# Two transformer blocks with self and cross attention: the opening of the kernel, with ScalarE's queue loading batch 1 and GpSimd normalising it

## The chip, the cores and the metric

The kernel runs on one core of one Trainium2 chip. The metric is the device time of one execution in microseconds (us). A core has five engines that run their own instruction streams side by side: TensorE (PE, matrix products), VectorE (DVE), ScalarE (ACT), GpSimd (POOL) and SyncE (SP), which here only starts transfers. They wait for each other through semaphores. Each stream is executed strictly in the order in which it was written, so what stands behind a waiting instruction waits too. A transfer (DMA) is started by an instruction in the stream of SP, ACT or POOL, and is then carried out by 16 DMA engines that all streams share.

## The reference

The input x has 4 batches of 512 tokens with 320 features each, and every batch has a context of 1601 tokens with 192 features. Two layers are applied, each with the same three blocks:

```
h1 = layernorm(x);  x = attention(h1, h1)      @ Wo + bo + x     # 20 heads of 16, self attention
h2 = layernorm(x);  x = attention(h2, context) @ Wo + bo + x     # cross attention, 1601 keys
h3 = layernorm(x);  a, g = split(h3 @ W1 + b1)
x  = (a * gelu(g)) @ W2 + b2 + x
```

A layernorm takes the mean and the variance of a token over its 320 features, multiplies by the inverse root and then applies a gain and a bias. An attention is softmax(q k / 4) v by heads. All of it is in float32.

## The kernel before, in words

**Tiles.** Tokens lie on 128 partitions, four blocks of 128 to a batch. A *unit* is one batch and one group of four heads, so a self attention has 4 x 5 units and unit 0 to 4 are batch 0, unit 5 the first of batch 1. For the scores, four heads share the array of TensorE, 32 rows each.

**The work of one self unit.** First its queries and keys are projected (`both`, L898, in two halves of 24 matmuls each). ACT copies the result out of PSUM. Each number is then split into a high and a low part (`split`, L825, two POOL instructions; unit 0 uses ACT and DVE instead, L919 and L920), and a transfer moves the parts to where the scores want them (`at_once`, L1609, runs the moves, L876: keys on SP's queue, queries alternating). Next come the *maxima*: four rounds of eight matmuls (L1076) into PSUM, with one DVE reduction (L1087) for each of the 16 tiles. `max_end` (L1152) turns these maxima into rows on DVE and sends them off with four small transfers (L1171, into `nrows`). Only then does the unit's *main part* run (`main`, L1311): four chunks c of keys, each with 12 matmuls for four heads (L1324, the third of each head adds the row of maxima), four exponentials on ACT (L1334), and the product with the values (L1350). The values themselves come from `values` (L1025, 24 matmuls for one chunk and one part of the heads).

**What sets the order.** The order of the instructions is written out by the Python program. In the main parts a planner does it: beside each chunk it gives out the following units' rounds of maxima (`give`, L1639), and after the chunk it takes projections, values and norms from chains by due times and a credit (`steps`, L487). A unit's maxima have to be finished by the chunk c = 1 of the unit before it; what is left by then is added as extra rounds. The eight PSUM banks are handed out by an estimate of when each comes free (`bank`, L413).

**The opening**, L1683 to L1724, is written out by hand, with `start["on"]` true. It loads x of batch 0, the first norm's gain and bias, the weights of queries, keys and values, two bias rows and x of batch 1, all on SP's queue, in this order. Ten warm-up matmul instructions (`warm(5)`, L431) run on TensorE meanwhile. Batch 0's norm follows: statistics on DVE (`stats`, L556), an inverse root by a bit trick and three Newton steps (`guess_root` L518, `better_root` L530, small DVE instructions on 128x4 numbers), the normalisation (`plain`, L620, twelve DVE instructions), and the turning by TensorE (`turn`, L634, twelve transposes and three copies out of PSUM that apply gain and bias; it ends with four POOL additions, `biased`, L617). Then come the projection of unit 0 and its transfer, the projection of unit 1, all of batch 1's statistics, root and normalisation on DVE, and then unit 0's maxima. Between its four rounds stand the two halves of unit 2's projection and some values. Two rounds of unit 1's maxima and four more sets of values end the opening; then unit 0's main part begins. Batch 1's turning is left to the planner, which places it after chunk c = 0 of unit 0.

Of the kernel before, what the change touches and what calls it, by code (L numbers as in the profile page):

```python
# [23 lines left out]
P = 128  # L24
# [54 lines left out]
def kernel(ctx: ExitStack, tc: tile.TileContext, x, context, ws, out):  # L79
# [96 lines left out]

    def load_x(b):

        src = x[b].rearrange("(c p) d -> p c d", p=P)

        def part(t):
            dma(out=xs[b][:, t], in_=src[:, t])
            loaded[b] = clock["round"] if t == NQ - 1 else 1 << 30

        return [lambda t=t: part(t) for t in range(NQ)]
# [38 lines left out]

    def load_row(t, v):
        dma(out=t, in_=v.rearrange("(o d) -> o d", o=1).to_broadcast([P, D]))

    def load_bias(l, i):
        if i > 2:
            l, i = l + 1, i - 3  # L230
        if l < L:
            load_row(brow[(3 * l + i) % 2], ws[l][("o1_b", "o2_b", "ff_b2")[i]])

# [283 lines left out]

    def guess_root(var):  # L518
# [6 lines left out]
        nc.vector.tensor_scalar(y.bitcast(I32), z.bitcast(I32), -1, 0x5F3759DF, ALU.mult, ALU.add)  # L525
# [4 lines left out]
    def better_root(h, y, z):  # L530


        eng = nc.vector if start["on"] else nc.gpsimd
        eng.tensor_tensor(z, y, y, ALU.mult)
        eng.tensor_tensor(z, z, h, ALU.mult)
        eng.tensor_scalar(z, z, 1.5, None, ALU.add)
        eng.tensor_tensor(y, y, z, ALU.mult)
# [13 lines left out]
    def add_norm(l, b, i, put, done, due):  # L551
# [13 lines left out]
        def root(step):  # L565
            if step == 0:
                s["root"] = guess_root(s["mv"][:, :, 1])
                s["rstd"] = s["root"][1]
            for _ in range(step + 1):
                better_root(*s["root"])  # L570
            s["round"] = clock["round"]
# [48 lines left out]
        def plain(t):  # L620
            if t == 0:
                s["hn"] = one.tile([P, DB, NQ, SLOT], F32, tag="hturned", name="hturned").rearrange("p k t w -> p (k t w)")
            for k, at, n in HK:
                w = n // SLOT
                (nc.vector if start["on"] else nc.gpsimd).tensor_scalar(
                    s["hn"][:, t * D + at : t * D + at + n].rearrange("p (d k) -> p k d", k=w),
                    xb[:, t, at : at + n].rearrange("p (k d) -> p k d", k=w),
                    s["mv"][:, t, 0:1], s["rstd"][:, t : t + 1], ALU.subtract, ALU.mult,
                )
            if start["on"]:  # L630
                busy("dve", 0.45)
            s["round"] = clock["round"]

        def turn(k, at, n):  # L634
            if k == 0:
                place()
            ps = bank("hps")
            for t in range(NQ):
                nc.tensor.transpose(ps[:n, t * P : (t + 1) * P], s["hn"][:, t * D + at : t * D + at + n], ident)
            written(0.5, ps)  # L640
# [511 lines left out]
    def max_end(u):  # L1152
# [14 lines left out]
        def rows():  # L1167
            for i in range(P // SLOT):
                part = slice(i * SLOT, (i + 1) * SLOT)
                queue = (nc.sync, nc.scalar, nc.gpsimd, nc.sync)[i] if start["on"] else nc.sync  # L1170
                queue.dma_start(out=slots[:, :, part], in_=turned[part, :])  # L1171
# [601 lines left out]
```

## Time and profile before

| | |
|---|---|
| median of 3 runs | 2921.99 us (2918.47 to 2926.42) |
| the profiled execution's own time | 2916.39 us |
| its span in the profile | 2914.6 us |
| TensorE busy | 2860.1 us (98% of the span) |
| DVE busy | 1975.7 us (68%) |
| ACT busy | 1950.2 us (67%) |
| POOL busy | 1299.4 us (45%) |
| mean granted TensorE clock | 0.995 |

The profile comes from one execution. A row of the timeline or of the chain of waits has a start and a duration in us, the engine, the line of the kernel and what was written from what. "x8" means that eight instructions were merged into one row. An engine name with a q (SPq, ACTq) is that engine issuing a transfer. A row of the windows has the stretch, its length, the busy time of PE, PEld (the loading of weights into the array), DVE, ACT and POOL, then the granted TensorE clock as a share of full speed, the busy share of the DMA engines and their rate. PE's busy time includes time in which a matmul is held up inside its queue, so "busy" is not "at full speed".

### The profile page before, as it was taken

The page shows a single profiled execution, that of the slowest core. Times are in us where ns is not written, and L with a number is a line of the kernel's source. Part 1 is how long each engine was busy: PE and PEld are TensorE (multiplying, and loading weights), DVE is VectorE, ACT ScalarE, POOL GpSimd, SP SyncE. Part 2 cuts the span into 40 slices and gives each one's busy share as a digit, 9 for nine tenths or more (in the row PEclk, how much of TensorE's full clock was granted, in tenths as well). Part 3 has the DMA queues.
Part 4 walks back from the last instruction along what each step waited for, and adds up shares of the span by engine and source line. Part 5 has one row for each costly group of instructions (what it writes and reads, how often), then busy time and mean ns, then how long its engine had stood idle before and what let it go on. Part 6 is the DMA issues. An engine that isn't in the chain of part 4 may idle for free.

```text
span 2914.6 us, 83287 instructions
## 1 busy us (share of the span) xinstructions
PE 2860.1 (98%) x35018; PEld 1545.0 (53%) x35018; DVE 1975.7 (68%) x3752; ACT 1950.2 (67%) x4033; POOL 1299.4 (45%) x1409
## 2 busy tenths in 40 slices
PE   8999999999999999999999999999999999999999
PEld 4445555555555555355554555555555555544554
DVE  7777888788788878323257678787778878862221
ACT  3777678888888888500138776788888888893000
POOL 3656345555645545211125653455455464551100
PEclk8999999999999999999999999999999999999999
DMA  4444223232132222200113432222221122122000
GB/s 106 114 121 102 72 71 97 58 89 60 48 96 59 55 54 63 85 17 11 36 45 88 109 99 67 61 64 57 54 66 47 50 73 60 45 65 67 23 21 13
DMA packets 163495, 188.59 MB, mean 65 GB/s; under 512 B 61989, under 2 KB 109105, under 8 KB 163121
## 3 DMA queue, kind: packets, MB, share of 16 engines
q1 hardware_dynamic: 162616, 181.69, 24.4%
q8 instruction: 275, 4.51, 0.6%
q10 hardware_dynamic: 472, 1.58, 0.2%
q14 instruction: 100, 0.81, 0.1%
q0 software_dynamic: 32, 0.00, 0.0%
HBM read 55.76 MB, written 29.36 MB: 29 GB/s over the span
## 4 chain that ended last, share of the span: by engine, by line
PE 88%; DVE 4%; POOL 4%; DMA 2%; issue 1%; ACT 1%; SPq 0%; POOLq 0%; ACTq 0%; DVEq 0%
PE av L1350 22%; PE st L1324 20%; PE fps L1435 10%; PE sps L1076 9%; PE yps L1542 6%; PE vps L1035 5%; PE kps L972 4%; PE ops L1250 3%; PE qkps L908 3%; PE fps L1495 3%; DVE nmax L1087 2%; PE qps L947 2%; PE sps L1101 1%; POOL o L1370 1%; DVE pm L1087 1%
## 5 line engine op out<-in xcount | busy, mean ns | idle before, releaser
L1334 ACT ACTIVATE pr<-st 128x512 f32<-128x512 f32 (+1 forms) x2720 | 1405.0, 603 | 321.4 <-PE st L1324 292.0
L1087 DVE TENSOR_REDUCE pm<-sps 128x1 f32<-128x512 f32 (+1 forms) x1920 | 1148.3, 660 | 244.6 <-PE sps L1076 239.0
L1370 POOL TENSOR_TENSOR o<-o,vo 128x512 f32<-128x512 f32 x576 | 739.9, 1285 | 930.3 <-ACT vo L1369 909.7
L1076 PE MATMUL sps<-kT,q 32*128 32x450 f32 (+1 forms) x4800 | 870.6, 422 | 8.1 <-DMA q<-halves 4.4
L1324 PE MATMUL st<-q,kT 32*128 32x512 f32 (+1 forms) x5120 | 788.9, 419 | 0.8 <-ACT o L1364 0.4
L1350 PE MATMUL av<-pr,vals 128*32 128x512 f32 (+1 forms) x5440 | 734.2, 606 | 27.3 <-ACT pr L1334 5.4
L1324 PEld LDWEIGHTS st<-q,kT 32*128 32x128 f32 (+1 forms) x5120 | 447.0, 180 | 293.0 <-issue 112.7
L1324 PE MATMUL st<-nrows,ones 32*128 32x512 f32 (+1 forms) x2720 | 560.6, 398 | 4.5 <-DMA nrows<-turned 4.4
L1087 DVE TENSOR_REDUCE nmax<-sps 128x1 f32<-128x512 f32 x640 | 397.2, 682 | 118.0 <-PE sps L1076 114.2
L1076 PEld LDWEIGHTS sps<-kT,q 32*128 32x128 f32 x4800 | 434.0, 184 | 67.1 <-ACT pr L1334 11.7
L1369 ACT COPY vo<-av 128x512 f32<-128x512 f32 x576 | 351.7, 611 | 14.7 <-PE av L1350 8.7
L1506 ACT ACTIVATE gl<-fps,b 128x512 f32<-128x512 f32 x80 | 54.8, 687 | 408.8 <-PE fps L1495 299.1
L1435 PE MATMUL fps<-hT,w 128*128 128x512 f32 x640 | 283.1, 597 | 0.0
L1350 PEld LDWEIGHTS av<-pr,vals 128*32 128x32 f32 (+1 forms) x5440 | 111.0, 108 | 300.3 <-DVE pm L1087 185.2
L1324 PEld LDWEIGHTS st<-nrows,ones 32*128 32x128 f32 (+1 forms) x2720 | 262.3, 180 | 14.5 <-DMA nrows<-turned 6.1
L1507 DVE SCALAR_TENSOR_TENSOR hid<-fps,b,gl 128x512 f32<-128x512 f32 x80 | 59.7, 748 | 248.1 <-ACT gl L1506 246.0
L1435 PEld LDWEIGHTS fps<-hT,w 128*128 128x128 f32 x640 | 119.2, 190 | 155.1 <-issue 152.2
L1542 PE MATMUL yps<-w,hid 128*128 128x320 f32 x640 | 175.7, 434 | 0.0
L1542 PEld LDWEIGHTS yps<-w,hid 128*128 128x128 f32 x640 | 120.5, 190 | 56.3 <-ACT gl L1506 5.3
L1250 PEld LDWEIGHTS ops<-wo,aT 112*32 112x32 f32 (+1 forms) x3072 | 98.2, 110 | 59.2 <-issue 28.5
L1250 PE MATMUL ops<-wo,aT 112*32 112x160 f32 (+1 forms) x3072 | 123.8, 299 | 3.7 <-POOL aT L1232 2.7
L1111 DVE TENSOR_REDUCE pm<-sps 128x4 f32<-128x508 f32 x160 | 98.9, 680 | 37.5 <-PE sps L1101 34.8
(89 smaller groups left out, 2453.7 us busy)
## 6 DMA issues: line engine op xcount, KB each, us to landing
kT<-stages SPq DMA_DIRECT2D x80, 400.5 KB
oway<-o SPq DMA_DIRECT2D x80, 256.0 KB
q<-halves SPq DMA_DIRECT2D x80, 256.0 KB
q<-halves SPq DMA_DIRECT2D x27, 512.0 KB
kT<-halves SPq DMA_DIRECT2D x40, 256.0 KB
aT<-oway SPq DMA_DIRECT2D x32, 224.0 KB
rT<-rway SPq DMA_DIRECT2D x32, 224.0 KB
hT<-hturned SPq DMA_DIRECT2D x96, 64.0 KB
```

What stands on the lines that cost most here:

```text
L972: nc.tensor.matmul(ps[(i * GT + f) * SLOT : (i * GT + f + 1) * SLOT, :w], lhsT=wk2[:, k, u.g * GD + f * SLOT : u.g * GD + (f + 1) * SLOT], ...
L1035: nc.tensor.matmul(ps[f : f + m, :w], lhsT=u.kvT[:n, k, at + f : at + f + m], rhs=wv[:n, k, h0 * DH : h1 * DH], start=(k == 0), stop=(k == ...
L1076: nc.tensor.matmul(own[0][:, :w], lhsT=u.queries(slice(j * SLOT, (j + 1) * SLOT), e, t), rhs=u.kT[j * SLOT : (j + 1) * SLOT, u.k0 + at : u ...
L1087: nc.vector.tensor_reduce(to, own[0][:, :w], AX.X, ALU.max)
L1250: nc.tensor.matmul(ps[f : f + m, : D // 2], lhsT=aT[:n, k, f * NQ + t * SLOT : f * NQ + t * SLOT + m], rhs=wo[:n, k, cols], start=(k == 0) ...
L1324: nc.tensor.matmul(own[0][:r, :], lhsT=ones[rows, :r] if e == 2 else u.keys(rows, c), rhs=u.rows[rows, :] if e == 2 else u.queries(rows, e ...
L1334: nc.scalar.activation(p[:r], own[0][:r], AF.Exp)
L1350: nc.tensor.matmul(ps[j * SLOT : (j + 1) * SLOT, :], lhsT=columns_of[:r, head : head + SLOT], rhs=pr.pop((c, j))[:r, :], start=True, stop= ...
L1369: nc.scalar.copy(vo, ps)
L1370: nc.gpsimd.tensor_tensor(u.o, u.o, vo, ALU.add)
L1435: nc.tensor.matmul(ps, lhsT=w1[:, k, i * FF + c * P : i * FF + (c + 1) * P], rhs=natural(u.hT[:, k]), start=start, stop=stop,)
L1542: nc.tensor.matmul(ps[:, :D], lhsT=hid[c][:, t * P : (t + 1) * P], rhs=w2[:, c, :], start=(c == 0), stop=(c == NHC - 1),)
```

## The change

Everything that changes is in the opening and in three helpers.

- The loads: x of batch 0 is started on SP's and ACT's queues in turn. x of batch 1 and the two bias rows are started on ACT's queue right behind. SP's queue goes from batch 0's tokens directly to gain, bias and weights. The four transfers of unit 0's row of maxima use SP and ACT only, two each (before: SP, ACT, POOL, SP).
- The root: on DVE, the last two instructions of a Newton step become one. For batch 1 the Newton steps run on POOL, with `guess_root`'s last instruction.
- The normalisation of batch 1 (`plain`) runs on POOL, and all three of its copies out of PSUM on ACT.
- The warm-up has seven matmuls, not five, and three small matmuls whose result nothing reads stand between the first four transposes of batch 0.
- The order: batch 1's statistics and root are written before unit 1's projection, and three sets of values behind it, before unit 1's transfer. Batch 1's normalisation follows that transfer. Unit 0's maxima then have unit 2's projection between them but no values. `max_end` of unit 0 stands ahead of unit 2's transfer. One round of unit 1's maxima is done in place of two, and batch 1's turning is done in the opening. Three sets of values and one round of maxima go over to unit 0's main part.

```diff
-    def load_x(b):
+    def load_x(b, queues=(nc.sync,)):
...
-            dma(out=xs[b][:, t], in_=src[:, t])
+            queues[t % len(queues)].dma_start(out=xs[b][:, t], in_=src[:, t])
...
-        eng = nc.vector if start["on"] else nc.gpsimd
+        eng = nc.vector if start["on"] and not b else nc.gpsimd
         eng.tensor_scalar(h, a, -0.5, None, ALU.mult)
...
+        eng = nc.vector if start["on"] and not b else nc.gpsimd
         eng.tensor_tensor(z, y, y, ALU.mult)
         eng.tensor_tensor(z, z, h, ALU.mult)
+        if eng is nc.vector:
+            eng.scalar_tensor_tensor(y, z, 1.5, y, ALU.add, ALU.mult)
+            return
...
-                (nc.vector if start["on"] else nc.gpsimd).tensor_scalar(
+                (nc.vector if start["on"] and not b else nc.gpsimd).tensor_scalar(
...
+            idle = bank("wps") if start["on"] and k == 0 and not b else None
             for t in range(NQ):
                 nc.tensor.transpose(ps[:n, t * P : (t + 1) * P], s["hn"][:, t * D + at : t * D + at + n], ident)
+                if idle is not None and t + 1 < NQ:
+                    nc.tensor.matmul(idle[:, :P], lhsT=ident, rhs=fill[:, :P], start=True, stop=True)
...
-            if start["on"] and k == 1:
+            if start["on"] and k == 1 and not b:
...
-                queue = (nc.sync, nc.scalar, nc.gpsimd, nc.sync)[i] if start["on"] else nc.sync
+                queue = nc.scalar if start["on"] and i % 2 else nc.sync
...
-    now(load_x(0))
+    now(load_x(0, (nc.sync, nc.scalar)))
+    now(load_x(1, (nc.scalar,)))
+    load_bias(0, 0, nc.scalar)
+    load_bias(0, 1, nc.scalar)
     now(load_self(0))
-    load_bias(0, 0)
-    load_bias(0, 1)
-    now(load_x(1))
...
-    warm(5)
+    warm(7)
...
     add_values(units[0])
+    for _ in range(NQ + 2):
+        run("norm")
     run("proj")
     run("proj")
-    for _ in range(2 * NQ + 2):
+    for _ in range(3):
+        run("values")
+    at_once(units[1])
+    for _ in range(NQ):
         run("norm")
-    at_once(units[1])
     add_proj(units[2])
...
-    for chain in ("proj", "proj", "values", None):
+    for chain in ("proj", "proj", None, None):
...
-    at_once(units[2])
-    run("values")
     max_reduce(first)
     max_end(first)
+    at_once(units[2])
+    second = units[1]
+    second.pairs = max_pairs(second)
+    round_of(second.pairs[0].popleft()[1] + second.pairs[1].popleft()[1])
+    for _ in range(3):
+        run("norm")
     loads.extend(load_x(2))
...
-    second = units[1]
-    second.pairs = max_pairs(second)
-    for _ in range(2):
-        round_of(second.pairs[0].popleft()[1] + second.pairs[1].popleft()[1])
-        run("values")
-        run("values")
```

More of the change, by code (lines that the diff above doesn't have):

```diff
@@ L223, in load_columns, with load_row, load_bias @@
         return [lambda c=c: column(*c) for c in chunks]
-    def load_row(t, v):
-        dma(out=t, in_=v.rearrange("(o d) -> o d", o=1).to_broadcast([P, D]))
-    def load_bias(l, i):
+    def load_row(t, v, queue):
+        queue.dma_start(out=t, in_=v.rearrange("(o d) -> o d", o=1).to_broadcast([P, D]))
+    def load_bias(l, i, queue=nc.sync):
         if i > 2:
@@ L231, in load_bias @@
         if l < L:
-            load_row(brow[(3 * l + i) % 2], ws[l][("o1_b", "o2_b", "ff_b2")[i]])
+            load_row(brow[(3 * l + i) % 2], ws[l][("o1_b", "o2_b", "ff_b2")[i]], queue)
     def load_norm(l, i):
@@ L516, in until, with guess_root @@
             run(name)
-    def guess_root(var):
+    def guess_root(var, b):
         a, h, y, z = (two.tile([P, NQ], F32, tag=f"root{i}", name=f"root{i}") for i in range(4))
@@ L525, in guess_root, with better_root @@
         nc.vector.tensor_scalar(y.bitcast(I32), z.bitcast(I32), -1, 0x5F3759DF, ALU.mult, ALU.add)
-        eng = nc.vector if start["on"] else nc.gpsimd
+        eng = nc.vector if start["on"] and not b else nc.gpsimd
         eng.tensor_scalar(h, a, -0.5, None, ALU.mult)
         return h, y, z
-    def better_root(h, y, z):
-        eng = nc.vector if start["on"] else nc.gpsimd
+    def better_root(h, y, z, b):
+        eng = nc.vector if start["on"] and not b else nc.gpsimd
         eng.tensor_tensor(z, y, y, ALU.mult)
         eng.tensor_tensor(z, z, h, ALU.mult)
+        if eng is nc.vector:
+            eng.scalar_tensor_tensor(y, z, 1.5, y, ALU.add, ALU.mult)
+            return
         eng.tensor_scalar(z, z, 1.5, None, ALU.add)
@@ L566, in root @@
             if step == 0:
-                s["root"] = guess_root(s["mv"][:, :, 1])
+                s["root"] = guess_root(s["mv"][:, :, 1], b)
                 s["rstd"] = s["root"][1]
             for _ in range(step + 1):
-                better_root(*s["root"])
+                better_root(*s["root"], b)
             s["round"] = clock["round"]
@@ L637, in turn @@
             ps = bank("hps")
+            idle = bank("wps") if start["on"] and k == 0 and not b else None
             for t in range(NQ):
                 nc.tensor.transpose(ps[:n, t * P : (t + 1) * P], s["hn"][:, t * D + at : t * D + at + n], ident)
+                if idle is not None and t + 1 < NQ:
+                    nc.tensor.matmul(idle[:, :P], lhsT=ident, rhs=fill[:, :P], start=True, stop=True)
+            if idle is not None:
+                busy("act", 0.0, idle)
             written(0.5, ps)
```

## The prediction

> **What bounds the kernel now.** I read the page first.
>
> ```profile
> span 2914.6 us, 83287 instructions
> PE 2860.1 (98%) x35018; PEld 1545.0 (53%) x35018; DVE 1975.7 (68%) x3752; ACT 1950.2 (67%) x4033; POOL 1299.4 (45%) x1409
> ```
>
> TensorE bounds nearly all of the span. The change touches nothing but the opening, so it can win only time that TensorE loses there. How much that is, the windows of the opening show (us; then PE, PEld, DVE, ACT, POOL busy; granted clock; DMA).
>
> ```profile
> 8.95:12.36 3.41, 1.18 (x4) 0.61 (x5) 3.34 (x14) 0.00 (x0) 0.00 (x0) 0.99 0.70 202
> 12.36:15.77 3.41, 3.41 (x25) 2.19 (x27) 1.10 (x3) 1.55 (x2) 0.00 (x0) 0.51 0.51 154
> 19.19:22.60 3.41, 1.13 (x24) 0.37 (x12) 3.17 (x10) 0.95 (x2) 3.33 (x5) 0.99 0.77 185
> 23.00:43.00 20.00, 18.23 (x184) 9.53 (x184) 17.97 (x47) 1.75 (x5) 4.29 (x6) 0.50 0.35 87
> 43.00:57.00 14.00, 13.45 (x184) 7.65 (x180) 10.52 (x19) 8.14 (x17) 1.68 (x3) 1.00 0.04 12
> ```
>
> The clock falls to half twice, each time behind a stretch of 3.4 us in which TensorE worked about a third of the time. The second fall lasts 20 us. In those 20 us DVE is busy for 17.97, so it holds TensorE up as well. The chain of waits says what comes first:
>
> ```profile
> 9.06 0.17 DVE root L537
> 9.52 2.60 DVE hturned L625 x9
> 12.17 2.11 PE hps L639 x9
> 14.27 3.50 PE qkps L908 x48
> 18.82 5.86 DMA q<-halves
> 24.77 1.23 PE sps L1076 x8
> ```
>
> DVE's root and normalisation, the turning, unit 0's projection and a transfer of 5.86 us lead to unit 0's first maxima at 24.77. The timeline has the rest:
>
> ```profile
> 25.33 3.39 DVE L625 TENSOR_SCALAR hturned<-x,mv,root 128x128 f32<-128x128 f32 x12
> 28.61 4.86 DVE L1087 TENSOR_REDUCE nmax<-sps 128x1 f32<-128x512 f32 x8
> 39.62 0.17 DVE L1155 TENSOR_REDUCE nmax<-nmax 128x16 fp32r<-128x16 f32 x1
> 40.29 1.45 SPq L1171 DMA_DIRECT2D nrows<-turned  x2
> 48.64 1.53 PE L639 MATMUL hps<-ident,hturned 128*128 128x128 f32 x12
> 49.49 2.11 ACT L647 ACTIVATE hT<-hps,lnb,lng 128x512 f32<-128x512 f32 x3
> 50.10 0.49 PE L1324 MATMUL st<-q,kT 32*128 32x512 f32 x2
> 52.28 1.06 PE L1350 MATMUL av<-pr,vals 128*32 128x512 f32 x8
> 53.28 0.74 PE L1076 MATMUL sps<-kT,q 32*128 32x512 f32 x8
> 53.95 2.80 PE L908 MATMUL qkps<-hT,wqk 128*32 128x256 f32 x48
> 54.05 2.48 DVE L1087 TENSOR_REDUCE nmax<-sps 128x1 f32<-128x512 f32 x4 [0.52 <-PE sps L1076]
> 56.68 0.49 PE L1324 MATMUL st<-q,kT 32*128 32x512 f32 x2
> ```
>
> Batch 1's normalisation holds DVE until 28.7, so the 16 reductions begin 3.8 us behind the first maxima. They end at 39.6. The scores of unit 0's chunk c = 1 start at 50.10, those of c = 2 at 56.68.
>
> **Where to measure.** By the planner's rules both kernels have done the same work when c = 2 begins. In the kernel before, the planner turns batch 1 behind c = 0. In the changed one that is done, and the credit goes to three sets of values; unit 3's projection isn't ready there in either, and follows behind c = 1. Of unit 1's maxima one round more is left, which `give` adds at c = 1 beside the extra round of unit 2 that the trace shows at 53.28. Units, rounds and due times are then equal, so I take the rest as unchanged, and the gain is 56.68 less the new start of c = 2.
>
> **Up to the first maxima.** Each small DVE instruction of the root takes 0.2 us from start to start (9.06 to 9.26 ends the last); three fewer save 0.6. The warm-up gets four matmul instructions on top of its ten:
>
> ```profile
> 1.53 6.48 PE L435 MATMUL wps<-fill,ident 128*128 128x512 f32 x10 [1.53 <-POOL scales L119]
> ```
>
> It ended at 8.0; four more are 2.6 at the row's mean and fewer at full clock, so it ends between 9.5 and 10.6, and with the three fillers TensorE is idle for little over 1 us ahead of the last transposes. I take it that the first fall of the clock goes. Nine transposes then cost 9 x 1.53/12 = 1.15 in place of 2.11 (saved 0.96), and 48 projection matmuls 2.80 in place of 3.50 (0.70). If the clock falls all the same, only 0.6 is left; the sum is 0.6 to 2.3. Against it stand the new neighbours on the DMA engines:
>
> ```profile
> 6.52 1.88 SPq L214 DMA_DIRECT2D wqk<-in_L_xattn_q_dram  x3
> 12.29 1.07 SPq L226 DMA_DIRECT2D brow<-in_L_xattn_o_b_dram  x2
> 17.58 3.35 POOL L618 TENSOR_TENSOR x<-x,brow 128x320 f32<-128x320 f32 x4 [11.17 <-DVE halves L920]
> ```
>
> SP issues the weights about 1 us earlier (two of batch 0's moves leave it, and an issue takes 0.63 here), but they now share the engines with batch 1's tokens and the bias rows. The latter were slow: issued at 12.29, first used at 17.58. Late weights cost 0 to 1.5; I take 0.3, since the last key weights (6.52 and six issues, less 1) are issued by 9.3 and wanted near 13. ACT's eight issues, by the same 0.63, end near 6, and ACT has nothing else to do until the turning, so they cost nothing. The transfer of 5.86 stays. First maxima: 24.77 - 2.26 + 0.3 = 22.8.
>
> TensorE has unit 1's projection and three sets of values ahead of them, so it is idle for about 2 us, where it was from 20.3 (19.19 and the 1.13 of that window) to 24.77.
>
> **Unit 0's maxima.** DVE is free by then. A reduction follows its matmuls by 0.8 (53.28 to 54.05), so the 16 run from 23.6 at 0.61 each (4.86 for eight), 9.8 in all, to 33.4; `max_end` takes 0.67 (39.62 to 40.29), to 34.1. Two row transfers on each queue take 1.45 to issue and some 1.8 to land, by the one landing that the view of transfers times:
>
> ```profile
> nrows<-turned POOLq DMA_DIRECT2D x1, 4.0 KB, 1.8
> ```
>
> The rows are there at 37.3.
>
> **POOL's chain.** This is what the change adds. Batch 1's later sisters show the durations on POOL:
>
> ```profile
> 96.38 0.20 POOL L534 TENSOR_TENSOR root<-root 128x4 f32<-128x4 f32 x1
> 96.66 0.20 POOL L535 TENSOR_TENSOR root<-root,root 128x4 f32<-128x4 f32 x1
> 104.01 4.39 POOL L625 TENSOR_SCALAR hturned<-x,mv,root 128x128 f32<-128x128 f32 x6
> 109.82 2.22 POOL L625 TENSOR_SCALAR hturned<-x,mv,root 128x128 f32<-128x128 f32 x3
> 111.92 0.62 POOL L827 CAST halves<-halves 128x512 fp32r<-128x512 f32 x1
> 112.63 1.28 POOL L828 TENSOR_TENSOR halves<-halves 128x512 f32<-128x512 f32 x1
> 115.13 2.25 POOL L625 TENSOR_SCALAR hturned<-x,mv,root 128x128 f32<-128x128 f32 x3
> ```
>
> The root's 13 instructions follow each other at 0.29, 3.8 in all. The normalisation is 4.39 + 2.22 + 2.25 = 8.9, where DVE took 3.39. A split is 2.0 (111.92 to the end at 113.91). What runs ahead of it and what it let go before:
>
> ```profile
> 21.80 1.11 DVE L525 TENSOR_SCALAR root<-root 128x4 int32<-128x4 int32 x1
> 22.92 0.57 ACTq L876 DMA_DIRECT2D q<-halves  x1
> ```
>
> DVE's third and last instruction of what stays on it of batch 1's root began at 21.80. It moves by 2, so POOL gets the root at about 19.9. POOL then runs: root to 23.7, split of unit 1 to 25.7, normalisation to 34.6, split of unit 2 to 36.5. Unit 1's transfer leaves 2.8 later than the 22.92 of before, and lands by 31.6, still ahead of its first maxima (banks come free near 31 to 33.6). Behind unit 2's split stands ACT: its queue holds unit 2's query transfer (0.6, to 37.1) and then batch 1's three copies out of PSUM (2.11, to 39.2). Only then are there enough banks for the first round of unit 0's main part, four tiles of scores and four of maxima. So POOL and ACT, not the rows at 37.3, set this start. In the kernel before, POOL was off this path.
>
> **From there to c = 2.** Round c = 0 ends at 40.1. Three sets of values follow: two of 192 columns and one of 128, by this row 2.14 and, by its columns, 0.71:
>
> ```profile
> 64.21 2.14 PE L1035 MATMUL vps<-wv,hT 128*32 128x192 f32 x48
> ```
>
> Together 2.9, to 43.0. Then c = 1 at its old 2.2 (50.10 to 52.28), the product with the values 1.0, unit 1's extra round 0.7, unit 3's projection 2.7, unit 2's extra round 0.7: 50.3. Before, that extra round stood ahead of the projection, which covered its four reductions (2.48). Now c = 2 follows directly and wants their banks, which I cost at 1.2. c = 2 begins at 51.5: a gain of 5.2 at full clock.
>
> **The clock behind the gap.** Between 31 and 39 TensorE has only one round of maxima and twelve transposes, some 2.5 us of work, less than the third of a window that went ahead of both falls. So I expect half clock at 39. It came back twice in the trace: after 3.4 us of steady work at 12.36, but only after 20 us from 23, where TensorE waited for DVE in every window. The values are a steady stream, so I take the shorter: 4 us at half clock, 2.0 lost. Bounds: 0 and 20 us, 0 to 10 lost. A rule that speaks here is in the Trainium skill, "TensorE: Matmul & The Clock Gate", in the part on the HAM clock gate: one idle window of about 3.4 us throttles, one busy window of the same length releases. By it the loss would be 1.7, an estimate. The first fall and its end agree with it; the 20 us do not, as TensorE counted as busy for 18.23 of them.
>
> **Sum.** 5.2 - 2.0 = 3.2. For the profiled execution that is 2916.4 - 3.2 = 2913.2. It stands 5.6 below the median of the runs, 2921.99, from which I take the same: 2918.8.
>
> **Rivals.**
> (1) The clock doesn't fall at 39, or the lost time is in waits anyway: the gain is 5.2 to 6.4 (without the stall at c = 2), 2916. For it speaks that c = 0 waits for ACT; against it, the light work from 31 on.
> (2) Slower: half clock stays, as it did from 23 to 43, because unit 0's main part starts with DVE one round of maxima behind and TensorE waits for it at c = 1. The gain of 5.2 is gone when it lasts more than 10.4 us; at 20 us the loss is 10, and the kernel is 4.8 slower, 2926.8. Against it: in the main parts from 43 on the clock was 1.00 throughout.
> (3) The change doesn't do what it says at the front: bias rows and tokens delay the weights by 1.5 and the first fall of the clock comes all the same. Then 2.3 - 0.6 + 1.2 = 2.9 are lost again and the gain is 0.3: 2921.7.
> (4) POOL isn't in the way, because the planner's bank choice doesn't tie the first scores to batch 1's copies. Then DVE alone bounds c = 2: 36 reductions and one `max_end` from 23.6, 36 x 0.61 + 0.7, to 46.3, and c = 2 some 0.8 later. The gain is 9.6: 2912.4.
> (5) POOL's and DVE's instructions hold each other up. One row speaks for it, the DVE root instruction at 21.80, which took 1.11 while POOL split unit 1's numbers, where its neighbours take 0.2. If each of batch 1's twelve POOL instructions held up a reduction by half of its 0.74, 4.4 would be lost on the maxima, of which 1.7 is slack up to POOL's own end: gain 0.5, 2921.5. Against it: reductions took the same 0.62 in the main part (2.48 for four from 54.05).
>
> **Chances.** The forecast has 0.50, (1) 0.18, (2) 0.10, (3) 0.09, (4) 0.08, (5) 0.05. The likeliest's own range is 2914 to 2923, three on either side for the weights and the clock, and 1.5 for the scatter of the runs. To hold eight in ten it takes in (4) and most of (2): 2911 to 2927. About 0.3%, 8.8 us, is what a measurement can tell from no change. Faster by more than that is (4) and the edge of (1): 0.14. Slower by more is the far half of (2): 0.07. The rest, 0.79, is the same.
>
> **What would show it.** First maxima near 22.8 with clock 1.0 up to there; 16 reductions in about 10 us from 23.6; POOL's normalisation in one piece to about 34.6; ACT's three copies ending near 39; then half clock for one or two windows, and c = 2 near 53.5. The first maxima later than 24 would prove the front part wrong, the scores of c = 0 before 38 POOL's chain, and a different count or order of instructions behind c = 2 the claim that the rest is unchanged.

## The result, and the profile after

The changed kernel takes 2916.82 us (median of 22 executions, 2912.39 to 2921.26), the kernel before 2922.64 us beside it (22 executions, 2913.86 to 2926.42). The ratio is 0.9982 with a 95% interval of [0.9975, 0.9988]. The difference of the means is 5.3 us (3.8 to 6.8). That is a small gain, clear of the noise, and within the 0.3% that the prediction called "the same". The forecast was 2918.8, a gain of 3.2, in a range of 2911 to 2927.

The two profiled executions tell the opposite: 2917.2 us for the changed kernel, 2916.39 for the kernel before. The latter was one of the fastest of its kernel, so the whole spans can't be set against each other, only places in them. The head of the page of the changed kernel:

```profile
span 2915.3 us, 83301 instructions
PE 2862.6 (98%) x35028; PEld 1548.6 (53%) x35028; DVE 1969.0 (68%) x3724; ACT 1951.2 (67%) x4033; POOL 1311.7 (45%) x1433
```

DVE lost 28 instructions and POOL got 24 more. All lines behind the first helper moved by 3 to 10: the maxima's matmuls are now L1084, their reductions L1095, the scores L1332, the values L1043. The opening, from the timeline:

```profile
1.53 8.16 PE L435 MATMUL wps<-fill,ident 128*128 128x512 f32 x14 [1.53 <-POOL scales L119]
12.75 5.44 PE L916 MATMUL qkps<-hT,wqk 128*32 128x256 f32 x96
...
22.49 1.22 PE L1084 MATMUL sps<-kT,q 32*128 32x512 f32 x8 [2.32 <-issue]
23.72 2.48 DVE L1095 TENSOR_REDUCE nmax<-sps 128x1 f32<-128x512 f32 x4 [4.05 <-PE sps L1084]
25.03 8.69 POOL L628 TENSOR_SCALAR hturned<-x,mv,root 128x128 f32<-128x128 f32 x12
26.92 7.27 DVE L1095 TENSOR_REDUCE nmax<-sps 128x1 f32<-128x512 f32 x12 [0.72 <-PE sps L1084]
33.62 0.61 POOL L835 CAST halves<-halves 128x512 fp32r<-128x512 f32 x1
34.32 1.27 POOL L836 TENSOR_TENSOR halves<-halves 128x512 f32<-128x512 f32 x1
34.89 1.45 SPq L1179 DMA_DIRECT2D nrows<-turned  x2
34.89 2.12 ACTq L1179 DMA_DIRECT2D nrows<-turned  x2
37.11 0.60 ACTq L884 DMA_DIRECT2D q<-halves  x1
37.76 2.11 ACT L655 ACTIVATE hT<-hps,lnb,lng 128x512 f32<-128x512 f32 x3 [8.90 <-DMA nrows<-turned]
38.59 0.79 PE L1332 MATMUL st<-q,kT 32*128 32x512 f32 x2 [3.38 <-ACT hT L655]
43.00 4.43 PE L1043 MATMUL vps<-wv,hT 128*32 128x128 f32 x72
```

The first maxima start at 22.49 (24.77 before), the normalisation runs on POOL in one piece, and ACT stands in its row transfers and one query transfer until 37.71 before it copies batch 1 out of PSUM. Unit 0's first scores wait for these copies. Where the chunks of unit 0 start shows in the chain of waits. Before (c = 0, 1, 2, 3):

```profile
46.41 0.43 PE st L1324 x2
...
50.17 0.42 PE st L1324
...
56.75 0.43 PE st L1324 x2
...
66.35 0.43 PE st L1324 x2
```

After (c = 1, the stall ahead of most of c = 2, c = 3; c = 0 is the row at 38.59 above):

```profile
47.43 0.42 PE st L1332 x2
...
54.15 1.29 DVE nmax L1095 x2
55.44 0.04 issue
55.48 0.73 PE st L1332 x3
...
64.89 0.43 PE st L1332
```

The lead is 7.8 us at c = 0, but the values come behind it now, and it is 2.7 at c = 1, 1.3 at c = 2 and 1.5 at c = 3.

This is one execution of each kernel, and others differ. Four profiles of the kernel before were taken in all, and three of the changed one; two of the four and two of the three are of the kernels cut off that come up below. In the chain of waits the four have c = 0 at 43.16 to 46.41 and c = 3 at 63.11, 64.70, 66.03 and 66.35, the three have c = 0 at 38.59 to 39.49 and c = 3 at 64.89, 66.13 and 66.86. So the lead at c = 0 is there in every pair, and at c = 3 it depends on the pair. Two of these rows, of the kernel before run once more and of the changed one cut off:

```profile
64.70 0.42 PE st L1324
```

```profile
66.86 0.42 PE st L1332
```

The windows of the opening on the grid of the clock (us; PE, PEld, DVE, ACT, POOL busy; granted clock; DMA):

```profile
19.09:22.50 3.41, 1.09 (x43) 0.85 (x36) 0.51 (x3) 0.68 (x3) 2.25 (x11) 0.99 0.61 165
22.50:25.91 3.41, 3.41 (x32) 1.48 (x32) 2.19 (x4) 0.00 (x0) 3.16 (x7) 0.51 0.02 5
25.91:29.33 3.42, 3.42 (x51) 1.65 (x43) 2.70 (x6) 0.95 (x2) 3.42 (x6) 1.00 0.88 211
29.33:32.74 3.41, 2.74 (x17) 1.25 (x16) 3.41 (x7) 0.00 (x0) 3.41 (x6) 0.99 0.06 19
32.74:36.15 3.41, 2.46 (x12) 1.96 (x10) 3.31 (x9) 0.00 (x0) 3.33 (x5) 0.50 0.00 0
36.15:39.57 3.42, 0.98 (x3) 0.57 (x3) 1.08 (x2) 1.81 (x3) 2.70 (x4) 0.50 0.47 77
39.57:42.98 3.41, 3.41 (x18) 1.67 (x17) 1.51 (x3) 1.67 (x4) 0.00 (x0) 0.50 0.76 207
42.98:46.39 3.41, 3.41 (x53) 2.55 (x56) 1.07 (x2) 1.06 (x3) 0.00 (x0) 0.51 0.02 5
```

The clock is at half for one window from 22.50 and for four from 32.74. Behind 68 us the order of the instructions on POOL, SP, DVE and ACT is the same in both kernels.

### The profile page after: what moved, and what is told of

The parts are those of the page before. It is cut to its first block, busy times and chain, and to the rows that moved or that the text cites. A ratio compares the mean times of both kernels' runs of the same rounds, so it can differ in the third digit from the quotient of the medians.

```text
span 2915.3 us, 83301 instructions
## 1 busy us (share of the span) xinstructions
PE 2862.6 (98%) x35028; PEld 1548.6 (53%) x35028; DVE 1969.0 (68%) x3724; ACT 1951.2 (67%) x4033; POOL 1311.7 (45%) x1433
## 4 chain that ended last, share of the span: by engine, by line
PE 87%; DVE 5%; POOL 4%; DMA 1%; issue 1%; ACT 1%; SPq 0%; ACTq 0%; POOLq 0%; DVEq 0%
PE av L1358 22%; PE st L1332 20%; PE fps L1443 10%; PE sps L1084 9%; PE yps L1550 6%; PE vps L1043 5%; PE ops L1258 4%; PE kps L980 3%; PE qkps L916 3%; PE fps L1503 3%; DVE nmax L1095 2%; PE qps L955 2%; PE sps L1109 1%; DVE pm L1095 1%; POOL o L1378 1%
## 5 line engine op out<-in xcount | busy, mean ns | idle before, releaser
L1095 DVE TENSOR_REDUCE pm<-sps 128x1 f32<-128x512 f32 (+1 forms) x1920 | 1149.0, 661 | 244.0 <-PE sps L1084 238.5
L1084 PE MATMUL sps<-kT,q 32*128 32x450 f32 (+1 forms) x4800 | 870.2, 421 | 6.1 <-issue 2.3
L1332 PE MATMUL st<-q,kT 32*128 32x512 f32 (+1 forms) x5120 | 792.0, 420 | 5.7 <-ACT hT L655 3.4
L1332 PEld LDWEIGHTS st<-q,kT 32*128 32x128 f32 (+1 forms) x5120 | 448.9, 180 | 299.0 <-ACT pr L1342 112.4
L1332 PE MATMUL st<-nrows,ones 32*128 32x512 f32 (+1 forms) x2720 | 561.2, 398 | 1.2 <-DMA nrows<-turned 0.8
L1095 DVE TENSOR_REDUCE nmax<-sps 128x1 f32<-128x512 f32 x640 | 397.0, 682 | 123.2 <-PE sps L1084 119.2
L1084 PEld LDWEIGHTS sps<-kT,q 32*128 32x128 f32 x4800 | 434.4, 183 | 64.9 <-ACT pr L1342 12.3
L1332 PEld LDWEIGHTS st<-nrows,ones 32*128 32x128 f32 (+1 forms) x2720 | 263.0, 180 | 10.8 <-DMA nrows<-turned 1.9
```

Of the source, the lines that this page charges most:

```text
L1084: nc.tensor.matmul(own[0][:, :w], lhsT=u.queries(slice(j * SLOT, (j + 1) * SLOT), e, t), rhs=u.kT[j * SLOT : (j + 1) * SLOT, u.k0 + at : u ...
L1095: nc.vector.tensor_reduce(to, own[0][:, :w], AX.X, ALU.max)
L1332: nc.tensor.matmul(own[0][:r, :], lhsT=ones[rows, :r] if e == 2 else u.keys(rows, c), rhs=u.rows[rows, :] if e == 2 else u.queries(rows, e ...
```

## The experiments

The theory going in: the steps of the prediction are right in kind, the gain of the opening is what the front and the new order save less what half clock takes, and nothing else changed. The first rival: the order is worth nothing, and only the front gains. The second: half clock is no loss, since TensorE waits anyway. A third came up when the profiles were compared: most of the gain lies behind the opening.

**The kernel before once more.** No edit. It shows what two equal kernels differ by, and whether the profiled execution was typical.

> The kernel before, unchanged, so that the granted clock of many of its executions can be set against that of the changed kernel (22 executions, mean clock 0.9953). In the two profiles at hand the changed kernel reaches c = 2 only 1.2 us earlier (55.48 against 56.68), yet the medians differ by 5.8. Theory 1, half clock: executions of the kernel before usually spend more time at half clock than the profiled one, by about 8 us (4 us of loss), so its mean clock is 0.992 to 0.993, and in a second profile the stretch at half clock that began at 22.6 ends later than 43, by one or more windows of 3.4 us. Theory 2, the path: the clock is 0.995 as in the changed kernel, and the difference shows in the start of c = 2 in a second profile, at 59 or later with the stretch ending at 43. Either way the ratio is 1.000.

Measured 2922.57 us, ratio 1.0004 [0.9995, 1.0013], with a mean granted clock of 0.9935. Its profiled execution took 2921.94 us, 5.5 more than the one of the prediction, on identical instructions. Beside the two falls of the opening it has falls at 191, 283 and 345 us, where the first had none. So the sum of the prediction was made against an execution that isn't typical of its kernel. Neither theory holds as it was put: the second stretch at half clock ended at 34.0 and not behind 43, and c = 2 started at 55.10, earlier than the 56.75 of the first profile and not at 59 or later.

**The two halves.** The front alone (loads on two queues, the shorter Newton step, `warm(7)` and the three fillers, in the old order and on the old engines), in part:

```diff
-    now(load_x(0))
+    now(load_x(0, (nc.sync, nc.scalar)))
+    now(load_x(1, (nc.scalar,)))
+    load_bias(0, 0, nc.scalar)
+    load_bias(0, 1, nc.scalar)
     now(load_self(0))
-    load_bias(0, 0)
-    load_bias(0, 1)
-    now(load_x(1))
...
-    warm(5)
+    warm(7)
```

> The kernel before with the front of the change alone: the loads on two queues, the shorter root of batch 0, seven warm-up matmuls and the fillers; order and engines of batch 1's norm as before. If the parts add up along one chain (my theory): first maxima at 22.5 in place of 24.77, reductions from 26.4 in place of 28.6, c = 2 about 2.2 earlier, ratio 0.9992. Rival, the front is the whole gain, because it keeps the clock up through unit 0's projection and the later order only moves waits: ratio 0.9982. Rival, nothing, because DVE's batch 1 norm takes up what is won: 1.000.

And the changed kernel with the old front put back, in part:

```diff
-    now(load_x(0, (nc.sync, nc.scalar)))
-    now(load_x(1, (nc.scalar,)))
-    load_bias(0, 0, nc.scalar)
-    load_bias(0, 1, nc.scalar)
+    now(load_x(0))
     now(load_self(0))
+    load_bias(0, 0)
+    load_bias(0, 1)
+    now(load_x(1))
...
-    warm(7)
+    warm(5)
```

> The changed kernel with the front of the kernel before (all loads on the first queue in the old order, five warm-up matmuls, no fillers, the longer root): batch 1's norm on GpSimd and the new order alone. If the parts add up: first maxima at 24.7, all of POOL's chain 2.2 later than in the changed kernel, c = 2 about 2 later than its 55.5, ratio 0.9990 (what is left of 0.9982 without the front's 2.2). Rival, the order is the whole gain: 0.9982. Rival, the order alone is a loss, since TensorE's light stretch of 31 to 39 costs more at half clock than the freed DVE gives: over 1.000.

Measured 0.999 [0.9981, 0.9999] and 0.9991 [0.9982, 1.0]. Together that is 0.9981, the whole change is 0.9982: the halves add as far as the intervals tell, and each is worth 2.6 to 2.9 us, though each alone is hardly told from nothing. The front alone has its first maxima at 22.50, the order alone at 24.34, so the 2 us of the first step come from the front. Where the order's gain lies these two runs don't show. In its profile c = 3 starts at 66.80, later than in any of the four of the kernel before (63.76 with the front alone). That the order alone gains nothing in the opening is not refuted by it: it also has the new queues of the row transfers, and a gain behind the opening that comes up below.

**Half clock.** The changed kernel with matmuls whose result nothing reads in the gaps of the opening, 18 of 512 columns in all:

```diff
     for _ in range(3):
         run("values")
+    warm(2)
     at_once(units[1])
...
         if chain:
             run(chain)
+        else:
+            warm(1)
...
+    warm(1)
     for _ in range(3):
         run("norm")
+    warm(4)
```

> The changed kernel with fillers (warm-up matmuls whose result nothing reads) where TensorE waits in the opening: two behind the three sets of values, one behind each of the last two rounds of unit 0's maxima and behind unit 1's round, four behind batch 1's turning. If half clock behind the light stretch is what costs (my theory, 2 us forecast, about 3.5 in the profile by the length of 39.9 to 46.2): the clock stays 1.00 from 23 on, c = 1 starts near 44 in place of 47.4, c = 2 near 52, ratio to the kernel before 0.997. Rival, the main part waits for DVE and ACT anyway: c = 2 at 55, ratio 0.9982. Rival, the fillers' bank holds up the maxima: slower than 0.9982.

Measured 2910.86 us, 0.9967 [0.9954, 0.9979], less than the changed kernel by 6.0 us of the medians (4.4 by the two ratios), at a mean clock of 0.998 in place of 0.9955. Its windows, and two rows of its timeline:

```profile
20.00:30.00 10.00, 9.61 (x96) 3.98 (x88) 6.80 (x12) 1.21 (x3) 9.08 (x20) 1.00 0.44 109
30.00:40.00 10.00, 9.69 (x71) 4.95 (x74) 7.11 (x15) 3.36 (x6) 8.72 (x12) 1.00 0.32 71
40.00:50.00 10.00, 9.83 (x165) 5.46 (x155) 7.12 (x12) 5.39 (x13) 1.00 (x2) 1.00 0.11 29
```

```profile
37.40 0.50 PE L1332 MATMUL st<-q,kT 32*128 32x512 f32 x2
39.47 2.82 PE L1043 MATMUL vps<-wv,hT 128*32 128x128 f32 x72
```

No half clock is left in the opening. The values take 2.82 us in place of 4.43 and start 3.5 us earlier, and most of c = 2 starts at 50.34 in place of 55.48. So half clock does cost, and the second rival falls. Fillers of the same kind, 22 of them, in the gaps of the kernel before:

```diff
     run("proj")
     run("proj")
+    warm(5)
...
         if chain:
             run(chain)
+        warm(1)
...
         run("values")
         run("values")
+        warm(1)
```

> The kernel before with fillers alone: five behind unit 1's projection, where TensorE waits for the transfer, one behind each of unit 0's four rounds of maxima and behind each of unit 1's two. Order, engines and loads as before. If DVE held TensorE up between 23 and 43 whatever the clock: reductions still begin at 28.6, the scores of c = 0 start near 44.5 in place of 46.3, and of the gain of the changed kernel with fillers (0.9967) less than half is there: ratio 0.9985 to 0.9995. Rival, the clock is the whole matter and order and engines are worth nothing: 0.997 or lower. Rival, fillers get in the way of the maxima: over 1.000.

Measured 2921.3 us, 0.9995 [0.9986, 1.0003]: nothing that can be told from no change. From 20 to 50 us the clock is at full there too. One of its windows, with the same columns:

```profile
30.00:40.00 10.00, 10.00 (x151) 5.10 (x155) 9.48 (x18) 1.01 (x3) 2.07 (x3) 1.00 0.33 80
```

DVE is busy for 9.48 of these 10 us, and c = 0 starts at 45.33, no earlier than in the four profiles of this kernel at half clock (43.09 to 46.34 in their timelines). Where DVE sets the pace, a faster TensorE waits more. The clock is worth something only in the changed kernel. DVE's busy time suggests that it is the normalisation taken off DVE that makes it so, but no run with fillers separates this from the new front.

**The normalisation back on DVE**, its Newton steps staying on POOL:

```diff
-                (nc.vector if start["on"] and not b else nc.gpsimd).tensor_scalar(
+                (nc.vector if start["on"] else nc.gpsimd).tensor_scalar(
```

> The changed kernel with batch 1's normalisation on DVE, the Newton steps still on POOL. If freeing DVE for the maxima is what the move to POOL is worth: DVE's 3.4 us stand ahead of the reductions, which begin near 26.5 in place of 23.7, the row transfers start near 37.5 in place of 34.9, the scores of c = 0 near 41 in place of 38.6: 2.4 lost, ratio 0.999. Rival, POOL's 8.7 us were the bound and DVE's are shorter: unit 2's split leaves earlier, c = 0 at 38 or earlier, ratio 0.998 or lower.

Measured 2921.68 us, 0.9994 [0.9986, 1.0003]: 4.9 us of the median are lost again (3.5 by the two ratios), up to twice the 2.4 that were expected. From its timeline, DVE's normalisation and the first reductions:

```profile
23.20 4.18 DVE L628 TENSOR_SCALAR hturned<-x,mv,root 128x128 f32<-128x128 f32 x12 [3.48 <-POOL root L540]
27.27 4.86 DVE L1095 TENSOR_REDUCE nmax<-sps 128x1 f32<-128x512 f32 x8
```

The reductions start at 27.27 in place of 23.72, and c = 0 at 42.12 in place of 38.59: the 3.5 us arrive in full. At c = 3 (69.54 in place of 64.89) it is 4.65. The work that POOL takes over in 8.69 us is worth having although DVE does it in 4.18. So for this part of the new order the first rival falls.

**The opening by itself.** Both kernels, cut behind the main parts of units 0 to 2. All later work is left out, and the tokens are stored as they are.

```diff
     for i, u in enumerate(units):
+        if i == 3:
+            flush()
+            for b in range(B):
+                for t in range(NQ):
+                    dma(out=out[b, t * P : (t + 1) * P, :], in_=xs[b][:, t, :])
+            break
```

> The kernel before, cut off behind the main parts of units 0, 1 and 2 (tokens are then written out as they stand, so most of the computation is left out): the opening by itself, many times. It is to be compared with the cut changed kernel, not with the whole one. Time near 110 us. If the change's 5.3 us arise in the opening and its half clock, the cut kernel before is 5 us slower than the cut changed one, with a mean clock that stands for 17 to 25 us at half clock against 14 to 17. If they arise later (fewer falls of the clock in the weeks of units behind, at 190, 280, 680 and 1500), the two cut kernels differ by only 0 to 1.5 us, as the two first profiles did at c = 3 (66.35 and 64.70 before, 64.89 after).

> The changed kernel, cut off in the same place and way. 5 us faster than the cut kernel before if the gain arises in the opening; 0 to 1.5 us faster if it arises later.

Measured 112.7 us on the mean of 6 executions (109.8 to 116.11) and 111.4 on the mean of 5 (109.82 to 113.25): 1.3 us less, with an interval from 1.0 more to 3.6 less, and not the 5 us of a gain made in the opening. The mean clocks of 0.862 and 0.895 make 31.1 and 23.4 us at half clock (twice the missing share of the time), 7.7 less. The two fastest executions are level (109.8 and 109.82). So the lead of the opening is not told from nothing, and it is less than the 5.3 us of the whole. The profiles are of the fastest execution of the one and the slowest of the other, with c = 3 at 63.11 and 66.86, which shows how little a single pair says. The version with fillers, cut in the same way:

> The version with fillers, cut behind the main parts of units 0 to 2 like the two short kernels before (what follows is left out, and the tokens are stored as they are). The uncut version has c = 3 at 59.75 us and no half clock ahead of it, 66.35 for the kernel before. If its gain of 9.7 us over the kernel before is made in the opening, the cut one is 6 to 8 us shorter than the cut kernel before (112.7 on the mean), 105 to 106.5, with a narrow spread of under 2 us, since the spread of the other two comes from where half clock falls in the opening. If the gain is later, it is only 2 to 3 us shorter.

Measured 106.2 us (4 executions, 105.99 to 106.31): 6.5 us below the cut kernel before (4.3 to 8.7), as expected, and 5.2 below the cut changed one (3.7 to 6.7). So what the fillers gain is gained in the opening. Their version scatters over 0.3 us, where the other two have 6.3 and 3.4: the scatter of the opening goes with the clock.

**A longer cut** of both, behind unit 21, some 480 us in, with the same text but for the number:

```diff
-        if i == 3:
+        if i == 22:
```

> The kernel before, cut behind unit 21's main part (some 400 us in), with the tokens stored as they are. Beside its twin of the changed kernel it tells where the gain of 5.3 us is made. Expected about 415 us, with a spread of some 8 us from run to run.

> The changed kernel with the same cut. Theory 1: the difference is made in the opening alone, 1.4 us by the short cuts, and the rest is scatter of the clock over the whole execution: 1.4 us below its twin, give or take 1.5. Theory 2: behind the opening the changed order also has fewer falls of the clock at 190, 285 and 341 us, where the profiles differ by 1.2 to 3 us: 4 to 6 us below its twin, with a higher mean granted clock.

Measured 484.4 us on the mean of 4 and 480.1 on the mean of 5: 4.3 us less (1.7 to 6.9). That speaks for theory 2, although its interval and that of the short cut overlap between 1.7 and 3.6. But not for its reason: the mean clocks (0.9623 and 0.9716) make 36.5 and 27.3 us at half clock, 9.3 less, hardly more than the 7.7 of the opening. (The length is some 65 to 70 us above what I had expected, a misjudged place of the cut.) What lies between the cuts, then? One thing is in every profile. At 331 to 345 us a row of maxima is sent behind the landing of another transfer. From the chain of waits of the two long cuts (before, after):

```profile
338.83 4.19 DMA nrows<-turned
```

```profile
337.81 3.01 DMA nrows<-turned
```

It takes 4.2 to 4.4 us in all five profiles with the old queues of unit 0's row transfers (4.18 in the one of the prediction), and 3.0 to 3.1 in all six with the new ones. TensorE waits for it (1.66 us before, 0.59 after), so 1.1 us are gained there in each. The instructions around it are the same. What differs ahead of it is, among other things, that the old kernel sends one of unit 0's rows through POOL's queue, which only those pages list among the queues (packets, MB, share):

```profile
q0 software_dynamic: 32, 0.00, 0.0%
```

Whether that is the cause was not tried: no run changes this queue alone.

More hangs on this place than the 1.1 us. These are SP's issues of the four transfers and of the next row's four, in the second profile of the kernel before and in the changed kernel:

```profile
335.12 3.79 SPq L1171 DMA_DIRECT2D nrows<-turned  x4
...
355.39 2.63 SPq L1171 DMA_DIRECT2D nrows<-turned  x4
```

```profile
336.26 3.93 SPq L1179 DMA_DIRECT2D nrows<-turned  x4
...
353.81 2.63 SPq L1179 DMA_DIRECT2D nrows<-turned  x4
```

From the one to the other it is 20.3 us here and 17.5 there. Over all profiles it is 18.5 to 21.4 in the five (20.4 on the mean) and 17.5 to 18.9 in the six (17.7). What exceeds the 1.1 us is a fall of the clock at 341 to 345 us, behind the longer wait: four of the five have it, and one of the six. Ahead of this place the new order loses something. From c = 3 to the first of the two issues the six take 270.4 us on the mean and the five 269.1, with more falls near 190 us (four of six, two of five) and at 276 to 288 us (five of six, three of five). With so few profiles, none of these counts is shown to come from the order and not from chance. Together 2.7 - 1.3 = 1.4 us are gained between the cuts by the profiles. The rest, 4.3 - 1.3 - 1.4 = 1.6 us, is smaller than the uncertainty of the three numbers.

**A better version.** ACT's queue ahead of c = 0 cut down: unit 2's query transfer (with that of its keys) behind batch 1's copies, one row transfer on ACT and three on SP, with the fillers (the last of them `warm(3)`):

```diff
-                queue = nc.scalar if start["on"] and i % 2 else nc.sync
+                queue = nc.scalar if start["on"] and i == 1 else nc.sync
...
     max_end(first)
-    at_once(units[2])
...
     for _ in range(3):
         run("norm")
-    warm(4)
+    at_once(units[2])
+    warm(3)
```

> The changed kernel with the fillers of the run before, and with ScalarE's share of the wait behind max_end cut down: unit 2's query transfer goes behind batch 1's three copies, and of the four row transfers ScalarE issues one and SyncE three. In the trace of the version with fillers ScalarE stands at row transfers (2.1 us for two), then the query transfer (0.6), then the copies (2.1), and c = 0 waits for the copies. If that queue is what sets c = 0, the copies end about 1.6 us earlier, then the row landing of SyncE's third transfer is next, some 0.6 us ahead of the old time: c = 0 near 36.8 (37.4), c = 3 near 59.1 (59.75), time 0.9965 of before. If the fillers' order or the rows on SyncE are next to wait for, c = 0 stays at 37.4 or later and the ratio at 0.9967 or above.

Measured 2908.94 us, 0.9952 [0.994, 0.9965]: faster than the kernel before and, by 7.9 us of the medians, than the changed one. Over the version with fillers the gain is 1.9 us by the means of different rounds (-0.5 to 4.3), which is not clear of nothing. From its timeline, the row transfers, the first copy and the first scores:

```profile
33.65 2.10 SPq L1179 DMA_DIRECT2D nrows<-turned  x3
33.65 1.45 ACTq L1179 DMA_DIRECT2D nrows<-turned  x1
35.15 0.78 ACT L655 ACTIVATE hT<-hps,lnb,lng 128x512 f32<-128x512 f32 x1 [7.79 <-DVE nmax L1095]
36.54 0.50 PE L1332 MATMUL st<-q,kT 32*128 32x512 f32 x2
```

ACT issues one row in place of two, the copies begin 1.3 us earlier than with fillers alone (36.42 there), and c = 0 at 36.54 in place of 37.40. So ACT's queue is what sets c = 0, and the effect there is a little larger than expected.

## Why the prediction was right, and where it was not

The time was right: 2918.8 against 2916.82, well inside the likeliest case's own range. The working was right in most of its steps and wrong in several sizes, and by its own place of measurement it was too high. That the time came out so near is in part luck, as the steps show.

- **First maxima at 22.8.** Measured 22.49. The warm-up ended at 9.69 (9.5 to 10.6 forecast), and weights were not late: the 96 projection matmuls ran from 12.75 in 5.44 us without a gap. The first fall of the clock is gone, as assumed (1.00 from 12.26 to 15.67). Rival (3) falls.
- **Reductions 23.6 to 33.4 at 0.61 each.** They began at 23.72 and took 0.61 each (7.27 for twelve), but ended at 34.19. I had put down about 2 us of idle TensorE ahead of the maxima and left it without a price. That window (1.09 of 3.41 busy) was as light as those that I had myself named ahead of both falls, and half clock followed at 22.50. It held back the second round's maxima: DVE waited 0.72 for them.
- **POOL's chain.** Normalisation 8.69 (8.9 forecast), split of unit 2 done at 35.59 (36.5). Rival (5) falls for the reductions: they took 0.61 with POOL busy beside them.
- **What stands ahead of the copies.** The step had ACT wait for POOL's split and end its copies at 39.2. ACT ended at 39.87, but POOL had been done for 1.5 us when ACT began the query transfer at 37.11. ACT was held up by its own two row transfers, 2.12 us behind `max_end`. I had costed them only as part of the landing of the rows, with the 1.45 us of SP's two, and not as time on ACT ahead of the copies. ACT's first took 1.44 us by itself, and the kernel before had the row that says so:

```profile
40.29 1.45 ACTq L1171 DMA_DIRECT2D nrows<-turned  x1
```

The number was right by luck, and the last version above shows what the queue is worth at c = 0. Rival (4) falls: c = 0 waited for the copies, though only for the first of the three, which ended at 38.55.
- **Half clock for 4 us behind the gap.** This is the term that was mis-sized most. It was 13.65 us, from 32.74 to 46.39, inside the bounds of 0 and 20. The price was 2.0; with the clock kept up by fillers c = 2 came 5.1 earlier, which is what this stretch and the one at 22.50 cost together. A rule of the Trainium skill had been weighed there ("TensorE: Matmul & The Clock Gate", Part 1 on the HAM clock gate), by which one busy window releases. By the busy time that isn't so: 39.57 to 42.98 counts as busy throughout, and the clock stayed at half behind it. The number of matmuls doesn't tell either: the window with 53 of them was the last at half, but so was the one at 22.50 with 32.
- **c = 2 near 53.5, a gain of 3.2.** The stall on DVE that I had costed at 1.2 was there (1.29 at 54.15), and most of c = 2 began behind it at 55.48: a gain of 1.3 in this pair. Other pairs differ, the second profile before has c = 2 at 55.10, so this size is not firm. The terms mis-sized are the half clock, the late second round of maxima and ACT's end, 0.7 later than forecast. Rival (2) had the half clock right (over 10.4 us), but its price wrong: TensorE waited for ACT in part of that time, and the kernel was not slower for it.
- **The rest unchanged.** In its order it is, in its time not. 1.1 us come from a transfer near 338 us in every profile, more from a fall of the clock behind it in some, and the rest, some 1.6 us by the long cuts, has no place. This term was put at nothing. So a gain of 1.3 at the place where I looked (by the short cuts from -1.0 to 3.6) and 5.3 by the runs gave a time near the forecast. Two errors of opposite sign met, and that is luck.
- **The median stands 5.6 above the profiled execution.** True for the kernel before, and not for the changed one, whose profiled execution lay 0.4 above its median. The forecast needed only the difference, so the offset did it no harm. But read from the two profiles alone, the change would be 0.8 us slower.
- **Rival (1)**, no fall of the clock, is what the version with fillers makes true: most of c = 2 starts at 50.34, 6.4 ahead of the first profile before, as the rival gave at most. The time is 10.6 us below the kernel before in the same round (2921.47; 9.6 by the ratio), more than that. By the cut version 6.5 of it are the opening's.

## What to carry to other kernels

Work taken off the engine that sets the pace shows only as far as the next holder lets it: here the lead of 7.8 us at c = 0 shrank to 1.3 at c = 2. Some 2.5 of that is work that moved behind c = 0 (with fillers 8.9 shrank to 6.4), and the rest is TensorE, now less busy, at half clock. After such a change look for windows with few matmuls, and fill them; fillers were worth nothing that could be told while DVE set the pace, and 4 to 6 us afterwards. On an engine that both issues transfers and computes, count each issue (0.6 to 1.4 us here) ahead of its next instruction. And don't compare two single profiles by their spans where executions of one kernel differ by more than the change: compare places, cut the kernel there, and let runs decide the sum.

## What the runs showed of the hardware

- The granted clock changes only on a grid of 3.413 us (22.50, 25.91, 32.74, 46.39 are 1, 3 and 7 steps apart from the first), and the grid lies differently in each execution: the kernel before fell first at 12.36 in one and at 13.5 in the other. The Trainium skill, "TensorE: Matmul & The Clock Gate", Part 1, calls the window free-running, and the two places of the grid agree; it puts the penalty of the ramp at under 1% of a typical kernel's span. Executions of one kernel lay between 2913.86 and 2926.42 here, 0.4% apart, and that is more than this whole change.
- A window need not be idle to bring the clock down. Those ahead of the falls had 1.09 busy us of 3.41 (1.18 and 1.13 in the kernel before), and 2.74 with only 17 matmuls. And one that counts as busy need not bring it back: in the kernel before, behind four such windows with 31 to 42 matmuls the clock stayed at half, and the one with 54 was the last. The count is no rule, though: other windows were the last at half with 25 (12.36 in the kernel before) and 32 (22.50 in the changed one). What the release goes by is open.

```profile
26.01:29.43 3.42, 3.42 (x31) 1.27 (x31) 3.42 (x12) 0.47 (x1) 0.00 (x0) 0.50 0.40 102
...
32.84:36.25 3.41, 3.41 (x42) 1.78 (x35) 2.41 (x5) 0.74 (x2) 1.88 (x2) 0.50 0.03 5
...
39.67:43.08 3.41, 3.41 (x54) 2.31 (x50) 2.90 (x7) 0.27 (x1) 2.49 (x4) 0.51 0.26 68
```

- Executions are slower by roughly 0.3 us for each us that they spend at half clock (the slope over the 22 of the changed kernel is 0.33, over the six of the cut kernel before 0.25), not by the half that the prediction counted.
- The same four row transfers took 1.1 us longer to land, 340 us in, in every profile with the old queues. The cause is open.
- Of two row transfers issued in a row, the first held ACT for 1.44 us and the second for 0.64; SP's two at the same time took 0.74 and 0.65.
